# Two layers of graph attention: the second half of a batch's masks and sums moved to later places in the hand-written order

## The chip, the cores and the metric

One core of one Trainium2 chip runs the kernel. The metric is the device time of one execution in microseconds, taken as the median of several runs. The kernel has 64 batches of 256 nodes with 512 features, all in float32. PE is the matrix engine, DVE the vector engine, ACT the scalar engine, POOL is GpSimd, and SP is the engine whose queue issues the DMAs.

## The reference

Layer 0 is a graph attention layer with additive scores; layer 1 is multi-head attention with eight heads of 64 and the same adjacency as mask. Both are behind a layer norm with ReLU and have a residual:

```
h = relu(layernorm(x));  H = h @ W                        # layer 0, W is 512 x 256
e = leaky_relu(H @ a[0] + (H @ a[1]).T, 0.2) + NEG * (1 - adj)
x = x + concat(softmax(e) @ H, H)
h = relu(layernorm(x))                                    # layer 1
q, k, v = h @ Wq.T + bq, h @ Wk.T + bk, h @ Wv.T + bv     # 8 heads of 64
s = where(adj == 0, -inf, q @ k.T / 8)
x = x + (softmax(s) @ v) @ Wo.T + bo
```

## The kernel before, in words

The fast path (`bounded`) computes softmax without subtracting a maximum: scores are bounded, so it takes exponentials, multiplies them by the 0/1 mask, and divides by the sum. Whether the bound holds is judged on the device at the end of the preparation.

Batches are taken in 32 groups g of two (b = 0 and 1). A group passes through four stages, and the stages of different groups run side by side:

- `first_norm` (g + 3): row statistics on DVE (`st`, `mv`), a pair of POOL instructions with a power (`factor`), the normalisation on ACT (`xn`, two tiles per batch), a 32x32 block transpose on DVE (`xt`), a DMA of the blocks to DRAM (`passed`), four DMAs back (`moved`), and a copy on ACT into `hT0`.
- `first_layer` (g + 2): `ph` on PE and its copy into `H` on ACT for four row tiles, with an addition `x<-H,x` on POOL for each; then four transposes `pn` on PE, the scores `e` on ACT and DVE, the products `po`, and the second norm with its own `xn`, `xt`, `passed`, `moved` and `hT1`. The last piece lets POOL make `sums` of `hT1` (`operand_sums`).
- `project` (g + 1): q, k and v by a scheme of seven products of half size each, so 21 products per group. PE writes `pq`, `pk` or `pv`. The intermediate `kept` tiles are copied out of PSUM by ACT into a ring of two buffers; a later addition on DVE reads such a tile, and frees its buffer. A product that adds to a bank waits until that bank was copied.
- attention of g: `scores` (l.716) makes eight `sc` on PE, eight exponentials on ACT into `p` (eight heads, one buffer), four multiplications by `maskT` on DVE (one for a pair of heads, l.735), and four additions on POOL that sum the two halves of the keys (l.736). `weigh` (l.744) makes from `p` the sums `total` and the products `pr`, DVE takes reciprocals `r` and `oT`, and `outputs` (l.777) does seven products `py`, each followed by an addition to `x` on DVE, and stores x.

The order of this work is written out by hand in `steps` (l.874), one string for each b. A letter takes one piece: S is `weigh` of the batch before and `scores` of this one, u a product of `project`, o one of `outputs`, s a piece of `first_layer`, n one of `first_norm`. At the middle letter of a string (l.897) come, for b = 0, the residual additions of `b_out` on POOL (`x<-x,b_out`, four) and the two `value_differences` (`v<-v`) on POOL, and for both b the load of x for g + 3. `scores`, `weigh` and the rest issue their DVE, ACT and POOL instructions as they are called; a scheduler then orders each engine's queue. `not_sooner` (l.123) forbids it to put an instruction ahead of the one issued before it on that engine, and PE's order is a chain throughout.

PSUM has five banks in turn (`mm`) and three that are held. `sc`, `total`, `pr`, `pn`, `ph`, `po` and the second products use the five in turn.

## Time and profile before

| what | value |
|---|---|
| runs before | 2572.51, 2575.55, 2576.94 us; median 2575.55 |
| the profiled execution | 2576.15 us, its span 2574.4 us, granted clock of PE 0.996 |
| DVE masks `p<-p,maskT` 128x1024 | 256, mean 1679 ns, 419.7 us |
| POOL sums `p<-p` 128x512 | 256, mean 1767 ns, 447.3 us |
| POOL `factor` with the power | 128, mean 712 ns |
| ACT exponentials `p<-sc` | 512, mean 609 ns |
| ACT normalisation `xn` | 256, mean 807 ns |
| SP: store of x | 64 of 512 KB, landing 3.1 us after issue |
| SP: `moved` | 496 of 128 KB, landing 3.4 us after issue |

The profile is one execution. The page gives for each engine its busy time and its share of the span; the view of waits says for which engine's work an engine stood idle, how much in total, how often, and the longest; the timeline gives instructions in order of time, merged where equal ones follow each other. All helpers record instructions under two lines (L35 for DVE, ACT and POOL, L137 and L140 for PE), so the names of the tiles tell the rows apart, not the lines. In names the numbers of group and batch are left out.

### The profile page before, as it was taken

Reading aid. Unit: us, or ns where it says so; the run is one execution under the profiler, and the core shown is the slowest. Engines: PE = TensorE matmul, PEld = TensorE weight load, DVE = VectorE, ACT = ScalarE, POOL = GpSimd, SP = SyncE. Lnnn points to the kernel's source line nnn. Section 1 sums busy time; section 2 is a strip of 40 time slices with the busy share of each in tenths; the row PEclk is TensorE's granted clock in tenths of the full one; section 3 lists DMA queues with packets and bytes.
Section 4 is the critical chain, followed back from the end, with each engine's and each line's share of the span. In section 5 each row is a group of like instructions: output and inputs, shape, how many; then the busy total and the mean of one; then the engine's idle time right before and its main releaser. Section 6 shows DMA issues by size and latency. Waiting matters only on the chain.

```text
span 2574.4 us, 41412 instructions
## 1 busy us (share of the span) xinstructions
PE 2508.6 (97%) x16158; PEld 2052.2 (80%) x16158; DVE 1856.3 (72%) x2971; ACT 1014.4 (39%) x2019; POOL 1069.4 (42%) x978
## 2 busy tenths in 40 slices
PE   8999999999999999999999999999999999999997
PEld 7778878888778788788787787887888887878885
DVE  6576766876767877767767678777677676687666
ACT  4443443343343443443433434434434344344321
POOL 3433444334444334443335443344443344433442
PEclk9999999999999999999999999999999999999999
DMA  5122122231232321222312323212223123222000
GB/s 184 66 83 78 55 90 82 91 99 50 74 99 74 99 85 56 82 91 82 99 58 66 99 74 99 85 60 79 91 82 99 64 61 99 83 91 91 33 25 34
DMA packets 129353, 205.40 MB, mean 80 GB/s; under 512 B 13952, under 2 KB 78208, under 8 KB 129152
## 3 DMA queue, kind: packets, MB, share of 16 engines
q1 hardware_dynamic: 129152, 202.69, 24.8%
q8 instruction: 129, 2.11, 0.3%
q14 instruction: 72, 0.59, 0.1%
HBM read 104.08 MB, written 98.57 MB: 79 GB/s over the span
## 4 chain that ended last, share of the span: by engine, by line
PE 87%; DVE 7%; ACT 3%; issue 1%; DMA 1%; SPq 1%; POOL 0%; ACTq 0%; DVEq 0%
PE pk L137 15%; PE py L137 14%; PE pv L137 14%; PE pq L137 13%; PE ph L137 9%; PE sc L137 8%; PE pr L137 7%; PE po L137 4%; DVE p L35 3%; PE total L137 2%; ACT p L35 1%; DMA moved<-passed 1%; DVE r L35 1%; DVE o_sums L35 1%; ACT kept_q L35 1%
## 5 line engine op out<-in xcount | busy, mean ns | idle before, releaser
L35 POOL TENSOR_TENSOR p<-p 128x512 f32<-128x512 f32 x256 | 447.3, 1767 | 528.6 <-DVE p L35 528.6
L35 DVE TENSOR_TENSOR x<-py,x 128x256 f32<-128x256 f32 x448 | 186.9, 417 | 345.1 <-PE py L137 338.6
L35 DVE TENSOR_TENSOR p<-p,maskT 128x1024 f32<-128x1024 f32 x256 | 419.7, 1679 | 0.0
L35 ACT ACTIVATE xn<-x,factor 128x512 f32<-128x512 f32 x256 | 194.4, 807 | 354.6 <-POOL factor L35 354.6
L35 ACT ACTIVATE p<-sc 128x512 f32<-128x512 f32 x512 | 263.2, 609 | 140.2 <-PE sc L137 140.1
L137 PE MATMUL sc<-q,k 64*128 64x256 f32 x2048 | 277.7, 394 | 10.4 <-ACT p L35 10.0
L137 PEld LDWEIGHTS sc<-q,k 64*128 64x128 f32 x2048 | 209.3, 186 | 79.4 <-ACT p L35 28.7
L137 PE MATMUL pq<-hT,wq_sb 128*128 128x256 f32 x1024 | 243.9, 386 | 22.2 <-ACT kept_q L35 22.2
L137 PE MATMUL py<-wo_sb,oT 128*128 128x256 f32 x1024 | 264.4, 381 | 0.4 <-DVE oT L35 0.4
L35 DVE RECIPROCAL r<-total 128x256 f32<-128x256 f32 x128 | 224.7, 1755 | 50.2 <-PE total L137 43.4
L137 PE MATMUL pk<-hT,wk_sb 128*128 128x256 f32 x1024 | 244.9, 382 | 0.0
L137 PE MATMUL pr<-p,v 128*32 128x256 f32 x4096 | 244.5, 379 | 0.0
L137 PEld LDWEIGHTS pq<-hT,wq_sb 128*128 128x128 f32 x1024 | 190.6, 191 | 67.1 <-ACT kept_q L35 33.0
L137 PE MATMUL ph<-w_sb,hT 128*128 128x258 f32 x1024 | 240.6, 383 | 0.3 <-ACT hT L35 0.3
L137 PE MATMUL pv<-wv_sb,hT 128*128 128x256 f32 x1024 | 237.5, 380 | 1.3 <-ACT kept_v L35 1.3
L35 POOL TENSOR_TENSOR factor<-factor,rexp 128x2 f32<-128x2 f32 x128 | 91.2, 712 | 354.4 <-DVE factor L35 354.4
L137 PEld LDWEIGHTS pk<-hT,wk_sb 128*128 128x128 f32 x1024 | 191.7, 190 | 36.1 <-issue 10.7
L137 PEld LDWEIGHTS ph<-w_sb,hT 128*128 128x128 f32 x1024 | 195.2, 191 | 29.9 <-ACT hT L35 0.9
L137 PEld LDWEIGHTS py<-wo_sb,oT 128*128 128x128 f32 x1024 | 195.4, 191 | 29.1 <-issue 1.1
L137 PEld LDWEIGHTS pv<-wv_sb,hT 128*128 128x128 f32 x1024 | 194.9, 190 | 28.6 <-ACT kept_v L35 1.7
L35 ACT COPY hT<-moved 128x512 f32<-128x512 f32 x248 | 141.1, 618 | 188.0 <-DMA moved<-passed 188.0
L137 PE MATMUL py<-wo_sb,o_sums 128*128 128x256 f32 x768 | 200.1, 384 | 8.4 <-DVE x L35 8.4
(122 smaller groups left out, 3789.5 us busy)
## 6 DMA issues: line engine op xcount, KB each, us to landing
passed<-xt SPq DMA_DIRECT2D x124, 512.0 KB, 3.0
moved<-passed SPq DMA_DIRECT2D x496, 128.0 KB, 3.4
x<-in_x_dram SPq DMA_DIRECT2D x64, 512.0 KB, 4.4
out_dram<-x SPq DMA_DIRECT2D x64, 512.0 KB, 3.1
wq_sb<-in_L_gnn_Wq_dram SPq DMA_DIRECT2D x2, 512.0 KB, 8.5
wk_sb<-in_L_gnn_Wk_dram SPq DMA_DIRECT2D x2, 512.0 KB, 10.4
wv_sb<-in_L_gnn_Wv_dram SPq DMA_DIRECT2D x2, 512.0 KB, 7.5
wo_sb<-in_L_gnn_Wo_dram SPq DMA_DIRECT2D x8, 128.0 KB, 4.0
```

The lines of the kernel that those rows point to most:

```text
L35: instruction = getattr(self.engine, operation)(*args, **kwargs)
L137: in_order(nc.tensor.matmul(*args, **kwargs))
```

## The change

The four masks with their four sums leave `scores` and become a generator of four pieces, `mask_pairs`. A new letter m takes one. In both strings two m follow S directly; the third and the fourth stand further back. The mask is now issued through `not_sooner`, too.

```
-            vector.tensor_mul(pair, pair, maskT[:, None, :, :].to_broadcast([P, 2, NT, N]))
-            not_sooner(
-                gpsimd, "tensor_add", pair[:, :, 0, :], pair[:, :, 0, :], pair[:, :, 1, :]
-            )
         places.extend((q_tag, k_tag))
         return p
+
+    def mask_pairs(p):
+
+        for i in range(HP):
+            pair = p[:, 2 * i : 2 * i + 2]
+            not_sooner(
+                vector, "tensor_mul", pair, pair, maskT[:, None, :, :].to_broadcast([P, 2, NT, N])
+            )
+            not_sooner(
+                gpsimd, "tensor_add", pair[:, :, 0, :], pair[:, :, 0, :], pair[:, :, 1, :]
+            )
+            yield
...
-    steps = ("Snuuuuonuouuossnunosunosnouso", "Sususuososuossusuonusonuouunous")
+    steps = ("Smmnuuuuonuouuomssnumnosunosnouso", "Smmsususuososuomssusumonusonuouunous")
...
-                parts = "Snn" + parts[2:].replace("uon", "unon", 1)
+                parts = "Smmnn" + parts[4:].replace("uon", "unon", 1)
...
+                elif part == "m":
+                    next(masks)
                 else:
                     waiting = (g, b, scores(g, b))
+                    masks = mask_pairs(waiting[2])
```

Without its four m the first string is the old one. The second has one s more than before, directly after S and the two m, so each piece of `first_layer` in b = 1 stands one place earlier, and the last s finds nothing left. The middle letter moves with the longer strings: in b = 0 it is now the first of the two s behind the third m.

In the built program the queues of a group in the middle of the run differ as follows.

- DVE, b = 0: the two transposes `xt` of the next norm stand between `o_sums` and the first mask, where they stood around the reciprocal before; two masks; then the additions of q and of three `py`; then masks 3 and 4; then the statistics `st`.
- DVE, b = 1: `o_sums` all stand ahead of the first mask (two masks stood among them); mask 3 stands after the third `py` addition, mask 4 after the v addition and the second pair of `xt`.
- POOL, b = 0: sums 1 to 3, one `x<-H,x`, the four residual additions, the two value differences, one `x<-H,x`, sum 4, the `factor` pair of `first_norm`, two `x<-H,x`. Before: sums 1 to 4, one `x<-H,x`, the `factor` pair, one `x<-H,x`, residual, value differences, two `x<-H,x`. In group 0 the `factor` pair stands ahead of sum 4, and from group 29 on there is none.
- POOL, b = 1: sums 3 and 4 stand behind the two `factor` pairs of the second norm.
- ACT: b = 0 is unchanged, with the two `xn` ahead of the fourth `H` copy; in b = 1 the last two `xn` of `first_norm` stand after the second `hT` copy, directly ahead of the exponentials, and the third and fourth `xn` of the second norm ahead of the first `kept_v`. In group 0, b = 1, both `hT` copies and these `xn` stand ahead of the last `kept_v`.
- SP, around the end of b = 1: `moved` of the second norm stands ahead of the store of x (behind it before), and three of the four `moved` of the next group ahead of the last `passed`; the load of x stands ahead of the last four `moved`.
- PE: the four `po` stand one place earlier among the products of b = 1; otherwise its order is the same.

## The prediction

> **What bounds the kernel now.** I read the page's busy shares first, then the waits of PE, then the timeline of a few groups. Columns of a timeline row: start, duration, engine, operation, out<-in, and in brackets the idle time before it with its releaser.

> ```profile
> span 2574.4 us, 41412 instructions
> PE 2508.6 (97%) x16158; PEld 2052.2 (80%) x16158; DVE 1856.3 (72%) x2971; ACT 1014.4 (39%) x2019; POOL 1069.4 (42%) x978
> ```
> PE is busy for all but 66 us. A gain can only come out of PE's idle time or out of a stage in which PE runs thin; a loss can come from anything that makes PE wait.

> ```profile
> PE pq L137 <- ACT kept_q L35: 22.2, 27, 0.9
> PE sc L137 <- ACT p L35: 10.0, 35, 0.8
> PE py L137 <- DVE x L35: 8.4, 2, 4.2
> ```
> The first row is one wait per group, in the first half (b = 0). The third is the last group, twice.

> ```profile
> 1275.73 2.56 PE L137 MATMUL sc<-q,k 64*128 64x256 f32 x18
> 1282.28 7.84 DVE L35 TENSOR_TENSOR p<-p,maskT 128x1024 f32<-128x1024 f32 x4
> 1290.04 0.68 DVE L35 TENSOR_TENSOR q<-pq,kept_q 128x512 f32<-128x512 f32 x1
> 1290.82 0.84 ACT L35 ACTIVATE kept_q<-pq,bq_sb 128x256 f32<-128x256 f32 x2 [4.01 <-DVE q L35]
> 1291.71 1.99 PE L137 MATMUL pq<-hT,wq_sb 128*128 128x256 f32 x8 [0.59 <-ACT kept_q L35]
> 1295.26 1.03 PE L137 MATMUL py<-wo_sb,o_sums 128*128 128x256 f32 x4
> 1296.67 0.68 DVE L35 BATCH_NORM_STATS2 st<-x 128x6 f32<-128x512 f32 x1
> 1300.95 4.96 POOL L35 TENSOR_TENSOR x<-x,b_out 128x512 f32<-128x512 f32 x4
> 1305.85 2.52 POOL L35 TENSOR_TENSOR v<-v 128x512 f32<-128x512 f32 x2
> 1308.48 0.37 ACT L35 COPY H<-ph 128x258 f32<-128x258 f32 x1 [2.54 <-PE ph L137]
> 1310.87 0.60 PE L140 MATMUL pn<-ident,H 128*128 128x128 f32 x4
> 1316.72 1.56 PE L137 MATMUL sc<-q,k 64*128 64x256 f32 x10
> ```
> One half-group, 1275.73 to 1316.72. Four masks hold DVE for 7.84 us; the q addition behind them frees a `kept` buffer; the third `kept_q` waits for that buffer, and PE waits for `kept_q`. Later POOL does the residual and value rows, and the last H copy ends at 1308.85, 2.02 us before PE's pn.

> ```profile
> 178.19 2.00 PE L137 MATMUL sc<-q,k 64*128 64x256 f32 x16
> 195.95 1.03 PE L137 MATMUL py<-wo_sb,o_sums 128*128 128x256 f32 x4
> 211.56 0.60 PE L140 MATMUL pn<-ident,H 128*128 128x128 f32 x4
> 217.41 1.56 PE L137 MATMUL sc<-q,k 64*128 64x256 f32 x10
> 255.19 1.99 PE L137 MATMUL sc<-q,k 64*128 64x256 f32 x15
> 2374.18 1.13 PE L137 MATMUL sc<-q,k 64*128 64x256 f32 x8
> ```
> Group 1 is undisturbed: 39.22 us for b = 0 (17.76 from sc to the third py, 15.61 to pn, 5.85 to the next sc) and 37.78 for b = 1, together 77.00. Groups 2 to 28 take (2374.18 - 255.19)/27 = 78.48 each. So 1.48 us per group can be won in b = 0.

> **The change part by part.** No instruction is added or removed; DVE, POOL, ACT and SP get other orders.

> *Two masks instead of four after the scores.* The q addition stands behind two masks. In the row above masks started 6.55 us after sc; in the built order the two transposes xt come before them (1.3 us), while the four o_sums, at 1.5 us each beside POOL's sums, shorten as sums start earlier (next item). By these rows the q addition comes about 8 us after sc instead of 14.3, and the third product whose `kept_q` needs the buffer ends only 10.7 us after sc. The wait goes.

> *b = 1 one piece earlier, and the hT rows fetched ahead of the store on SP.* The rows moved1 no longer stand behind the store that waits for a py addition, so the hT copy (1276.77 here, after 4.80 us of idling for its DMA, with the exponentials right behind it) needs DMAs issued some 3 us earlier: passed is issued at 1263.99 and lands in 3.0, moved in 3.4 (page), so at 1270.4. The copy then follows the v copy (ends 1271.97) and ends 2.7 us before sc; xn (1.52 us) ends 1.2 before it, and the exponentials start 1.16 after it, as in group 1. The passed rows of the next group move the other way on SP, behind the masks' transposes: about 7 us later. With 3.0 and 3.4 us to land they are there some 12 us after sc (wanted by their hT copy at 22), the last quarter of the other half at 9.5 (wanted at 12), and the load of x in between on SP lands in 4.4, some 10 us before its statistics. Covered. With both items b = 0 runs like group 1: -1.48 x 27 = -40.0 us.

> *Masks 3 and 4 behind the third py addition: a new chain to pn.* On POOL, the third sum now stands before the residual rows, the fourth sum behind the value rows, and the pow pair of the next norm behind that. ACT has xn before the last H copy, and the fourth pn transpose needs that copy. Worked from py (= a): mask 3 starts at a+1.41, where the statistics start now. How mask pairs and sums run back to back is shown in b = 1:

> ```profile
> 1325.83 2.35 DVE L35 TENSOR_TENSOR p<-p,maskT 128x1024 f32<-128x1024 f32 x2
> 1327.12 3.42 POOL L35 TENSOR_TENSOR p<-p 128x512 f32<-128x512 f32 x2 [1.83 <-DVE p L35]
> ```
> The first of these sums takes 2.19, the second 1.26. So sum 3 lets its successor start 3.45 after mask 3. Then POOL, start to start: H row 0.60, residual and value rows 7.36 (1300.95 to 1308.31), H row 0.69, sum 4 1.22, pow pair 0.97: a+15.70. Then ACT: 0.03 to xn, 1.43 to the copy of H, 0.37, and 0.05 to PE: a+17.58. PE wants the fourth transpose at a+15.61+0.33 = a+15.94. New wait: 1.64; the first matmul after a wait takes 0.1 more (1.99 for 1.89 in the pq row): 1.74 us. It is in groups 1 to 28 (in group 0 the pow pair stands ahead of sum 4; from 29 on there is no norm): +1.74 x 28 = +48.7 us. Bounds: 0.8, if sum 3 got ahead of mask 4 and took 1.26; 2.7, if sum 4 too were held for 0.93. I take 1.74, from rows of the same pairs. Behind the waiting xn on ACT stand the H copy, kept_k and the e rows, which keep their distance from pn; behind the waiting xt on DVE stand two py additions, the later needed 0.3 us after it ends.

> The trace decides who waits: mask 4 starts before mask 3 ends, and sum 3 pays 0.93. [...]

> *Masks 3 and 4 in b = 1.* They stand among the v addition and the xt transposes. By the rows' durations sum 4 ends 26 us after sc, wanted at 33, and the first kept_v ends 1.5 us before PE's third pv: nothing.

> *Ends.* Group 29 gains 1.4 and has no chain. Group 30 gains 1.3, but its value rows come at a+12.3 where pr wants them at 10.3: +0.8 net. Group 31 waits 4.2 us twice for DVE x behind four masks; with two masks the addition comes as PE arrives, and the slow matmuls after the wait go too (2.07, 1.91 and 1.87 for 1.03). A wait of 1.6 behind masks 3 and 4 comes instead: about -8.7 for both halves. Group 0: in b = 1 ACT now has the second hT copy before the last kept_v, which delays it by about 3 us: +2.5.

> *Sum.* -40.0 + 48.7 - 1.4 + 0.8 - 8.7 + 2.5 = +1.9 on the profiled execution's 2576.15, which is 0.6 above the median of 2575.55: 2577.5 against that median.

> **The rivals.** 0.2% is 5.15 us, about what a measurement of this kernel can tell from no change.

> *The wait at pn lowers PE's clock (slower).* A wait of 2.69 us was followed by eight matmuls at half rate:

> ```profile
> 86.57 3.05 PE L137 MATMUL pv<-wv_sb,sums 128*128 128x256 f32 x8 [2.69 <-ACT kept_v L35]
> 89.41 2.57 PE L137 MATMUL pv<-wv_sb,hT 128*128 128x256 f32 x8
> 2529.00:2531.00 2.00, 1.56 (x4) 1.29 (x5) 0.81 (x3) 0.00 (x0) 2.00 (x2) 0.50 0.00 0
> ```
> The last row is a stretch after a 4.21 us wait; its granted clock (third figure from the end) is 0.50. Waits of 1.1 and 1.3 us (160.8 and 169.2) were followed by full rate. So the point lies between 1.3 and 2.7, and 1.64 may pass it. Price: 8 x 0.215 = 1.7 us per group, +48: 2626; in half the groups 2602.

> [...]

> *The gain stays away (slower).* If xn, now directly before the exponentials, or a late DMA holds them, b = 0 keeps half of its 1.48: +20, 2598; all of it: 2618. Against it: 2.4 us of slack on ACT between xn and the exponentials.

> *No wait at pn, or half of it (faster).* If sum 3 gets in first: 0.93 x 28 less, 2551. If the pow pair does not hold ACT at all: 2577.5 - 48.7 = 2529. Against it: POOL's order is fixed in the program and its rows repeat to 0.02 us in groups 2 to 28.

> *Nothing moves.* The built orders do move; only if all terms are hidden: 2575.

> **How the numbers follow.** Main case 2577.5, own range 2566 to 2590 (a tenth of a microsecond in the chain is 2.8 us): 0.46, of it 0.07 faster, 0.24 same, 0.15 slower. Clock: 0.14. Gain away: 0.18. Faster rival: 0.18, of it 0.01 same. Nothing moves: 0.04, of it 0.03 same, 0.01 slower. Faster 0.24, same 0.28, slower 0.48. The range leaves a tenth on each side: 2550, as the lower half of the faster rival lies below, and 2614, as the full price of the clock and of the missing gain lie above.

> **What would show it.** Right: the row pq <- kept_q gone from PE's waits; a row pn <- ACT H in its place, some 28 times, 1.4 to 1.8 us each, about 45 us; 17.8 us from sc to the third py in every group; xn on ACT waiting for POOL factor; the py <- DVE x waits of the last group below 2 us. Wrong: no pn wait (the chain is shorter), pn waits followed by a granted clock of 0.5 (clock rival), or sc and pq waits still there (gain away). A wait at pv or at ph in the steady groups would be one that I have not seen.

## The result and the profile after

| | median | runs |
|---|---|---|
| before, same chip | 2574.82 us | 2572.51 to 2576.94 (4) |
| after | 2572.10 us | 2571.69 to 2574.16 (4) |

The ratio is 0.9991, with a 95% interval of 0.9974 to 1.0009: no change that can be told from none. The profiled execution of the changed kernel took 2571.85 us (span 2570.2, granted clock 0.998), 4.3 less than the one before. First the head of its page, then its waits of PE (in total, times, longest).

```profile
span 2570.2 us, 41394 instructions
PE 2490.8 (97%) x16158; PEld 2052.6 (80%) x16158; DVE 1691.7 (66%) x2971; ACT 1012.5 (39%) x2019; POOL 1008.7 (39%) x978
```
```profile
PE pn L140 <- ACT H L35: 41.2, 29, 1.5
...
PE sc L137 <- ACT p L35: 8.0, 31, 0.3
PE pv L137 <- ACT kept_v L35: 7.8, 3, 4.9
PE py L137 <- DVE x L35: 3.1, 2, 1.7
```
The row pq <- kept_q (22.2 us) is gone; a row pn <- ACT H, once in each of groups 0 to 28, has taken its place. The half-group that the prediction showed of before, now of after (timeline: start, duration, engine, operation, and in brackets the idle time ahead with its releaser):

```profile
1278.71 3.92 PE L137 MATMUL sc<-q,k 64*128 64x256 f32 x32
...
1283.72 2.32 DVE L35 TENSOR_TENSOR p<-p,maskT 128x1024 f32<-128x1024 f32 x2
...
1286.39 0.69 DVE L35 TENSOR_TENSOR q<-pq,kept_q 128x512 f32<-128x512 f32 x1 [0.35 <-PE pq L137]
...
1296.48 1.03 PE L137 MATMUL py<-wo_sb,o_sums 128*128 128x256 f32 x4
...
1297.89 2.35 DVE L35 TENSOR_TENSOR p<-p,maskT 128x1024 f32<-128x1024 f32 x2
1299.25 2.12 POOL L35 TENSOR_TENSOR p<-p 128x512 f32<-128x512 f32 x1 [10.86 <-DVE p L35]
...
1301.92 4.94 POOL L35 TENSOR_TENSOR x<-x,b_out 128x512 f32<-128x512 f32 x4
...
1309.97 1.26 POOL L35 TENSOR_TENSOR p<-p 128x512 f32<-128x512 f32 x1
...
1311.19 0.70 POOL L35 TENSOR_TENSOR factor<-factor,rexp 128x2 f32<-128x2 f32 x1
...
1312.20 1.52 ACT L35 ACTIVATE xn<-x,factor 128x512 f32<-128x512 f32 x2 [6.46 <-POOL factor L35]
...
1313.62 0.35 ACT L35 COPY H<-ph 128x258 f32<-128x258 f32 x1
...
1314.03 0.32 PE L140 MATMUL pn<-ident,H 128*128 128x128 f32 x1 [1.44 <-ACT H L35]
...
1319.60 1.56 PE L137 MATMUL sc<-q,k 64*128 64x256 f32 x10
```
The scores run without a stop (3.92 us), and the q addition comes as soon as PE has its product. Then the new chain: mask 3, sum 3, residual and value rows, sum 4, factor, xn, H, and PE's fourth pn 1.44 us late. Per group 2 to 28 the first sc stand 78.64 us apart, 78.48 before. From the third py on, b = 0 takes 1.66 us more (from pn to the next sc 7.51, before 5.85). Without it a group would take 76.98: so 1.50 was won, and 1.66 lost.

### The profile page after: what moved, and what is told of

Read it like the earlier page. It is cut to its first block, busy times and chain, and to the rows that moved or that the text cites. A ratio compares the mean times of both kernels' runs of the same rounds, so it can differ in the third digit from the quotient of the medians.

```text
span 2570.2 us, 41394 instructions
## 1 busy us (share of the span) xinstructions
PE 2490.8 (97%) x16158; PEld 2052.6 (80%) x16158; DVE 1691.7 (66%) x2971; ACT 1012.5 (39%) x2019; POOL 1008.7 (39%) x978
## 4 chain that ended last, share of the span: by engine, by line
PE 77%; POOL 14%; DVE 3%; issue 3%; ACT 2%; DMA 1%; POOLq 0%; SPq 0%; DVEq 0%; ACTq 0%
PE pq L137 15%; PE pv L137 15%; PE py L137 12%; PE sc L137 10%; PE pk L137 9%; PE pr L137 8%; POOL x L35 6%; PE po L137 4%; POOL p L35 4%; POOL v L35 3%; PE total L137 2%; DVE p L35 2%; ACT xn L35 1%; POOL factor L35 1%; PE ph L137 1%
## 5 line engine op out<-in xcount | busy, mean ns | idle before, releaser
L35 POOL TENSOR_TENSOR p<-p 128x512 f32<-128x512 f32 x256 | 407.8, 1603 | 970.9 <-DVE p L35 881.0
L35 ACT ACTIVATE p<-sc 128x512 f32<-128x512 f32 x512 | 264.0, 612 | 211.2 <-PE sc L137 203.3
L35 ACT ACTIVATE xn<-x,factor 128x512 f32<-128x512 f32 x256 | 194.4, 806 | 387.1 <-POOL factor L35 387.1
L35 DVE TENSOR_TENSOR x<-py,x 128x256 f32<-128x256 f32 x448 | 186.4, 416 | 243.8 <-PE py L137 234.6
L35 DVE TENSOR_TENSOR p<-p,maskT 128x1024 f32<-128x1024 f32 x256 | 301.5, 1209 | 0.0
L137 PE MATMUL sc<-q,k 64*128 64x256 f32 x2048 | 266.5, 390 | 8.0 <-ACT p L35 8.0
L35 DVE RECIPROCAL r<-total 128x256 f32<-128x256 f32 x128 | 224.8, 1756 | 66.3 <-PE total L137 59.9
L137 PE MATMUL py<-wo_sb,oT 128*128 128x256 f32 x1024 | 262.8, 379 | 3.5 <-DVE x L35 3.1
L137 PEld LDWEIGHTS sc<-q,k 64*128 64x128 f32 x2048 | 213.0, 186 | 62.1 <-issue 25.9
L35 DVE STREAM_TRANSPOSE xt<-xn 128x512 f32<-128x512 f32 x248 | 164.4, 692 | 134.2 <-ACT xn L35 134.2
L137 PE MATMUL pr<-p,v 128*32 128x256 f32 x4096 | 245.5, 379 | 0.4 <-POOL v L35 0.4
L137 PE MATMUL pk<-hT,wk_sb 128*128 128x256 f32 x1024 | 244.9, 382 | 0.0
L137 PE MATMUL pv<-wv_sb,hT 128*128 128x256 f32 x1024 | 238.6, 381 | 4.9 <-ACT kept_v L35 4.9
L137 PE MATMUL pq<-hT,wq_sb 128*128 128x256 f32 x1024 | 239.9, 382 | 0.0
L137 PE MATMUL ph<-w_sb,hT 128*128 128x258 f32 x1024 | 239.4, 381 | 0.3 <-ACT hT L35 0.3
L137 PEld LDWEIGHTS pv<-wv_sb,hT 128*128 128x128 f32 x1024 | 195.3, 191 | 32.2 <-ACT kept_v L35 5.3
L137 PEld LDWEIGHTS pk<-hT,wk_sb 128*128 128x128 f32 x1024 | 191.7, 190 | 36.1 <-issue 10.7
L137 PEld LDWEIGHTS pq<-hT,wq_sb 128*128 128x128 f32 x1024 | 191.8, 190 | 35.0 <-issue 9.9
L137 PEld LDWEIGHTS py<-wo_sb,oT 128*128 128x128 f32 x1024 | 193.8, 190 | 32.3 <-DVE x L35 3.9
L137 PEld LDWEIGHTS ph<-w_sb,hT 128*128 128x128 f32 x1024 | 194.4, 190 | 29.6 <-ACT hT L35 0.9
L137 PEld LDWEIGHTS pr<-p,v 128*32 128x32 f32 x4096 | 133.3, 110 | 88.6 <-POOL v L35 0.9
L35 POOL TENSOR_TENSOR factor<-factor,rexp 128x2 f32<-128x2 f32 x128 | 91.7, 716 | 281.2 <-DVE factor L35 281.2
## 6 DMA issues: line engine op xcount, KB each, us to landing
wk_sb<-in_L_gnn_Wk_dram SPq DMA_DIRECT2D x2, 512.0 KB, 10.7
```

What stands on the lines that cost most here:

```text
L35: instruction = getattr(self.engine, operation)(*args, **kwargs)
L137: in_order(nc.tensor.matmul(*args, **kwargs))
```

## The experiments

Each kernel is measured beside the kernel before on the same chip. Where a string has a new letter R, the work of the middle letter (residual additions, value differences, the load) stands at R, so that it keeps its place when letters ahead of it move. (In b = 1 of the two kernels without the additional s, R, which there moves only the load, stands two letters ahead of the old middle; the order on SP is that of the kernel before all the same.) The string of group 0 is fitted in the same way. "b = 0" and "b = 1" are the two strings; times per group are means of groups 2 to 28, from one first sc to the next.

### Which part brings the 1.50 us

Four kernels differ only in the strings. All four masks back behind S in b = 0:

```
-    steps = ("Smmnuuuuonuouuomssnumnosunosnouso", "Smmsususuososuomssusumonusonuouunous")
+    steps = ("SmmmmnuuuuonuouuossRnunosunosnouso", "SmmsususuososuomssuRsumonusonuouunous")
```

> All four masks of b = 0 stand directly behind S again, the middle letter's work where it was before the change; b = 1 as in the changed kernel. It separates the two items of the gain. If the gain of 1.48 us per group comes from the second string alone (hT copies and xn earlier, exponentials on time): scores in 3.85 us, no pq wait although four masks stand ahead of the q addition, no pn wait, 76.98 us per group; with 4.5 us back in the last group about 2530 us. If the two masks carry the larger part, as the prediction's first item has it: the pq <- kept_q wait of 0.8 us is back in 27 groups, about 2552 us.

Measured: 2533.19 us, ratio to before 0.9839 (0.9825 to 0.9852). The profile has 77.01 us per group, 3.85 from the first sc to the next product in every group, and neither a pq <- kept_q nor a pn row. Four masks ahead of the q addition hurt nobody once the exponentials are on time; the gain needs nothing from the first string.

The other way round: b = 0 as in the changed kernel, b = 1 as before.

```
-    steps = ("Smmnuuuuonuouuomssnumnosunosnouso", "Smmsususuososuomssusumonusonuouunous")
+    steps = ("SmmnuuuuonuouuomsRsnumnosunosnouso", "SmmmmususuososuossRusuonusonuouunous")
```

> b = 0 as in the changed kernel (two masks, then two later); the string of b = 1 and its four masks as before the change, without the additional s. If the second string frees the scores: sc is late again by a mean of 0.70 us as before (4.55 for 3.85), pq <- kept_q stays away because only two masks stand ahead, the pn wait of 1.66 stays: 2572 + 27 x 0.70 + 4.5 for the last group, about 2595 us. If the masks of b = 0 carry the whole gain: 3.85 us for the scores, 2576 us.

Measured: 2589.32 us, ratio 1.0054 (1.0039 to 1.0070). The pq wait stays away, the scores are late again (3.86 to 5.35 us, mean 4.36 for 3.85), the pn wait stays: 79.17 us per group. ACT ahead of the scores, in the timeline of this kernel:

```profile
1285.55 1.14 ACT L35 COPY hT<-moved 128x512 f32<-128x512 f32 x2 [4.85 <-DMA moved<-passed]
1286.59 4.00 ACT L35 ACTIVATE p<-sc 128x512 f32<-128x512 f32 x8
```
PE has begun its sc at 1284.46, and the exponentials stand behind an hT copy that waits for its DMA. So two masks alone take away the pq wait, but not this delay.

The second string holds two edits, the additional s and the later masks 3 and 4. The s alone, with four masks behind S in both strings:

```
+    steps = ("SmmmmnuuuuonuouuossRnunosunosnouso", "SmmmmsususuososuossuRsuonusonuouunous")
```

> Nothing of the masks moves: all four stand directly behind S in both halves, as before the change. Only the one s more in the second string is left of it. If that s is the whole gain: groups 2 to 28 at 76.98 to 77.00 us with scores in 3.85 us, no pq wait, no pn wait, and about 2533 us as with four masks in the first half alone. If masks 3 and 4 behind o_sums in b = 1 carry part of it (four masks at up to 1.96 us ahead of the reciprocal ri in b = 1): scores or pk late in b = 1, 0.5 us or more per group, 2547 us or more.

Measured: 2585.54 us, ratio 1.0041 (1.0027 to 1.0055): slower than before by 0.4%. b = 0 is at its 39.22 us, but b = 1 takes 39.34 for 37.79, so that a group takes 78.56, as good as before; groups 0 and 1 lose 8.1 and 1.5 us on top (89.17 and 78.54 for 81.10 and 77.01). The waits of PE, then DVE, ACT and PE in one b = 1 of this kernel:

```profile
PE pv L137 <- ACT kept_v L35: 45.7, 33, 5.0
```
```profile
1330.48 6.77 DVE L35 TENSOR_TENSOR p<-p,maskT 128x1024 f32<-128x1024 f32 x4
1337.17 0.15 DVE L35 RECIPROCAL ri<-po 128x1 f32<-128x1 f32 x1
...
1347.28 1.52 ACT L35 ACTIVATE xn<-x,factor 128x512 f32<-128x512 f32 x2 [2.33 <-POOL factor L35]
1348.70 0.56 ACT L35 COPY kept_v<-pv 128x512 f32<-128x512 f32 x1
...
1349.32 1.99 PE L137 MATMUL pv<-wv_sb,sums 128*128 128x256 f32 x8 [1.21 <-ACT kept_v L35]
```
The same place in the kernel with the split masks in b = 1 (four_masks_first_half; its scores begin at 1295.89, here at 1325.53):

```profile
1314.23 1.52 ACT L35 ACTIVATE xn<-x,factor 128x512 f32<-128x512 f32 x2 [0.47 <-POOL factor L35]
1315.66 0.56 ACT L35 COPY kept_v<-pv 128x512 f32<-128x512 f32 x1
...
1317.90 1.89 PE L137 MATMUL pv<-wv_sb,sums 128*128 128x256 f32 x8
```
The additional s puts the last two xn of the second norm ahead of the first kept_v on ACT. With four masks in front, DVE reaches the second norm's statistics late (the reciprocal ri ahead of them starts 11.64 us after sc, with two masks 7.52), and this kept_v starts 23.17 us after sc; with two it starts at 19.77, ahead of PE's pv at 22.01. So the later masks pay for the earlier piece. The fourth combination, later masks without the s:

```
+    steps = ("SmmmmnuuuuonuouuossRnunosunosnouso", "SmmususuososuomssRusumonusonuouunous")
```

> Masks 3 and 4 of b = 1 stand later as in the changed kernel, but the second string has no additional s, and b = 0 has its four masks directly behind S. With it the four combinations in b = 1 are complete. If the s is needed (the moved rows then still stand behind the store of x on SP, and the hT copy ahead of the exponentials is late): scores at 4.0 to 5.4 us and the pq wait of 0.8 us as before the change, 78.5 us per group, about 2573 us. If the later masks alone are enough, because DVE reaches the second norm some 2.4 to 4 us earlier: 3.85 us, 77.0 us per group, about 2533 us.

Measured: 2576.38 us, ratio 1.0007 (0.9998 to 1.0016). Scores late by a mean of 0.80 us, the pq wait back (17.4 us), 78.71 per group. SP in this kernel, then in the changed one, a little ahead of the scores of b = 0 (they begin at 1276.96 and 1278.71):

```profile
1265.74 0.38 SPq L35 DMA_DIRECT2D passed<-xt  x1
1271.39 0.40 SPq L823 DMA_DIRECT2D out_dram<-x  x1
1271.89 3.13 SPq L457 DMA_DIRECT2D moved<-passed  x4
```
```profile
1264.28 0.34 SPq L35 DMA_DIRECT2D passed<-xt  x1
1267.82 1.73 SPq L457 DMA_DIRECT2D moved<-passed  x4
1273.13 0.40 SPq L823 DMA_DIRECT2D out_dram<-x  x1
```
Without the s, the four moved are issued behind the store of x, 6.2 us after passed, and the hT copy idles 4.81 us for them; with it they are issued 3.5 us after passed, ahead of the store. Over the whole run ACT's hT copies wait 12.6 us for DMA in the changed kernel, 199.5 here.

Together, with four masks behind S in b = 0:

| b = 1 | no additional s | additional s |
|---|---|---|
| four masks behind S | 2574.8 (before) | 2585.5 |
| masks 3 and 4 later | 2576.4 | 2533.2 |

Neither edit is worth anything alone; the two together are worth 41.6 us.

### What the wait at pn hangs on

Only mask 4 of b = 0 one letter on, behind the factor pair (the first string alone is shown):

```
-    steps = ("Smmnuuuuonuouuomssnumnosunosnouso",
+    steps = ("Smmnuuuuonuouuomssnunmosunosnouso",
```

> Only mask 4 of b = 0 moves one letter on, so that sum 4 (1.22 us) stands behind the factor pair on POOL and sum 3 stays ahead of the residual rows. My theory (the chain is sum 3, residual, value, sum 4, factor, xn, H copy): the wait shrinks from 1.66 by 1.22 to about 0.45, 28 x 1.2 less: 2538 us. Rival (it is a single late thing such as sum 3 held by mask 4, or the DVE statistics): the wait stays whole (2572) or goes whole (2526).

Measured: 2544.44 us, ratio 0.9883 (0.9868 to 0.9898). The pn row shrinks from 41.2 to 11.1 us; from pn to the next sc it is 6.43 us, so 0.58 of the 1.66 are left. Sum 4 was worth 1.08 us in the chain (1.22 expected). By subtraction the rest is sum 3 ahead of the residual rows; the next kernel moves that one too.

Masks 3 and 4 both behind the factor pair (again the first string):

```
-    steps = ("Smmnuuuuonuouuomssnumnosunosnouso",
+    steps = ("Smmnuuuuonuouuossnunmmosunosnouso",
```

> Masks 3 and 4 of b = 0 stand together behind the statistics and the factor pair instead of ahead of them; b = 1 as in the changed kernel. My theory (the wait at pn comes from sums 3 and 4 ahead of the factor pair on POOL): the pn wait of 1.66 us goes in groups 1 to 28, 78.64 - 1.66 = 76.98 us per group, 2572.1 - 28 x 1.66 = 2526 us. Rival (a wait takes its place, because the py7 and pk additions now stand behind two masks of 1.21 us): 0.5 to 2.4 us per group come back, 2540 to 2593 us, with a row py <- DVE x or pk <- ACT kept_k in PE's waits.

Measured: 2555.30 us, ratio 0.9922 (0.9909 to 0.9936). The pn wait is gone and b = 0 has its 39.22 us, but b = 1 takes 38.67 for 37.76. A wait did take its place, though not the one I had named. Waits, and the place in the timeline of this kernel:

```profile
PE sc L137 <- DVE r L35: 16.5, 27, 0.7
PE sc L137 <- DVE oT L35: 15.8, 27, 0.6
```
```profile
1303.94 1.78 POOL L35 TENSOR_TENSOR x<-H,x 128x256 f32<-128x256 f32 x2
...
1304.00 2.26 DVE L35 SCALAR_TENSOR_TENSOR e<-e 128x512 f32<-128x512 f32 x2
1306.19 1.75 DVE L35 RECIPROCAL r<-total 128x256 f32<-128x256 f32 x1
```
The same DVE pair in the kernel with four masks first:

```profile
1291.88 1.38 DVE L35 SCALAR_TENSOR_TENSOR e<-e 128x512 f32<-128x512 f32 x2
```
Sum 4 now delays the last two H rows of POOL, and they meet the e rows on DVE. Side by side both took longer than in the kernel with four masks first (the e rows 2.26 us for 1.38, the H rows 1.78 for 1.32). The reciprocal behind them is 0.88 late, and the scores of b = 1 wait twice for it and its product, 0.58 us each.

### How near the clock rival was

POOL gets two more instructions behind sum 3 of b = 0, so that pn waits longer. They add the second half of the keys to a sum and take it off again (`mask_pairs` is given b for it). The three kernels differ in the slice (`:, 0, k, :P`, then `:, 0, k, :`, then `:, :, k, :`):

```
+            if b == 0 and i == HP - 2:
+                half, other = (pair[:, 0, k, :P] for k in range(2))
+                not_sooner(gpsimd, "tensor_add", half, half, other)
+                not_sooner(gpsimd, "tensor_sub", half, half, other)
```

> The changed kernel with two POOL instructions of 128 x 128 behind sum 3 of b = 0, about 0.35 us each by half of those of 128 x 256, so that the wait at pn is about 2.15 us, between the 1.45 of the changed kernel (matmuls at full rate behind it) and the 2.82 with two of 128 x 256 (total and pr at half rate behind it, 1.6 us more). If the limit lies above 2.15: 2572.1 + 28 x 0.7 = 2592 us. If it lies below: 28 x 1.6 = 45 us more, 2637 us.

> The changed kernel with two more POOL instructions of 128 x 256 (the second half of one head is added to its sum and taken off again) behind sum 3 of b = 0, 0.6 us each by the H rows, so that the wait at pn grows from 1.45 to about 2.7 us. If a wait of this size leaves the granted clock alone: 2572.1 + 28 x 1.2 = 2606 us, with the matmuls behind pn at 0.215 us of 128x256 for two. If it halves the clock for eight matmuls, as behind the 2.69 us before pv in the kernel before: 1.7 us more per group, 2654 us.

> The same with two instructions of 128 x 512, 1.22 us each by sum 4: the wait at pn grows to about 3.9 us. Without a change of the clock: 2572.1 + 28 x 2.44 = 2640 us. With eight matmuls at half rate behind each wait: 48 us more, 2688 us, and a granted clock of about 0.5 in the stretch behind pn.

| | pn wait | groups 1 to 28 with slow matmuls behind it | mean cost of these in all 28 | time |
|---|---|---|---|---|
| changed kernel | 1.45 us | 0 | 0 | 2572.1 |
| 128 x 128 twice | 2.27 | 16 | 0.94 us | 2625.0 |
| 128 x 256 twice | 2.82 | 24 | 1.41 | 2659.7 |
| 128 x 512 twice | 3.90 | 28 | 1.95 | 2711.0 |

The cost is the time from the fourth pn to the next sc above the 5.57 us that it takes in the changed kernel. Where it is paid it is 1.63 to 1.69 us for waits of 2.27 and 2.82. Longer waits and slow matmuls together give 28 x (0.82 + 0.94) = 49, 28 x (1.37 + 1.41) = 78 and 28 x (2.45 + 1.95) = 123 us; 53, 88 and 139 were measured, and most of the rest of the last is in groups 0, 30 and 31, which take 6.8, 4.4 and 2.7 us more than in the changed kernel. With the shortest pause, two groups that follow each other, each after a wait of exactly 2.27; first the timeline, then the stretches behind pn (length, busy time, and third from the end the granted clock):

```profile
215.47 0.32 PE L140 MATMUL pn<-ident,H 128*128 128x128 f32 x1 [2.27 <-ACT H L35]
...
217.63 2.96 PE L137 MATMUL pr<-p,v 128*32 128x256 f32 x32
```
```profile
296.57 0.32 PE L140 MATMUL pn<-ident,H 128*128 128x128 f32 x1 [2.27 <-ACT H L35]
...
298.14 1.91 PE L137 MATMUL pr<-p,v 128*32 128x256 f32 x32
```
```profile
216.00:218.00 2.00, 2.00 (x16) 0.59 0.62 252
```
```profile
297.00:299.00 2.00, 2.00 (x28) 1.00 0.58 231
```
The price was as the rival had it, and the waits at which it began lie between 1.45 and 2.27 us; but there was no one length. The same wait of 2.27 us cost 1.6 us in one group and nothing in the next, and the share of the groups that paid grew with the wait, from 0 to 16, 24 and 28 of 28.

The records of the granted clock in the traces show what decided. In each of the twelve, every drop of the granted clock starts on a grid of steps of 3.413 us, and lasts one step or two (the last one runs into the end of the trace). In the kernel before, the five drops start 6, 709, 7 and 6 steps apart; in the changed kernel the three start 24 and 703 apart. The grid lies elsewhere in each execution: the first drop starts 87.35 us into the span before, 85.25 after. Here are the steps of the grid, called windows, that hold the two waits, each with the window behind it:

```profile
212.94:216.35 3.41, 1.15 (x8) 1.00 0.00 0
216.35:219.76 3.41, 3.41 (x30) 0.50 0.78 303
```
```profile
291.44:294.86 3.41, 2.86 (x15) 1.00 0.00 0
294.86:298.27 3.41, 1.70 (x17) 1.00 0.12 50
298.27:301.68 3.41, 3.41 (x72) 1.00 0.69 259
```
The first wait lies within one window: PE idles for 2.26 of 3.41 us, and the next window has half the clock. The second is cut in two, 0.55 and 1.71 us, and nothing follows. Between the first sc and the last product the twelve traces hold 93 windows at full clock that a window at half clock follows; each has 1.92 us of idling or more. The 8510 that one at full clock follows have 1.88 or less. (In the kernel before and the changed one alone, 4 windows with 2.49 to 3.30 us, and 1438 with up to 1.66.) So in these traces it was the idling within a window that counted. By these figures a wait of 1.45 us by itself was too short wherever it fell, one of 3.90 left at least 1.95 in one window however it was cut, and for those between it depended on where the grid cut them.

### A version without the wait

Only in the last group was the split of b = 0 worth something. So: four masks behind S everywhere, two and two in b = 0 of the last group.

```
+            if g == NG - 1 and b == 0:
+                parts = "SmmnuuuuonuouuomsRsnumnosunosnouso"
```

> As with four masks in the first half, but in the last group b = 0 takes two masks and then two, as in the changed kernel. In the last group the split is worth what the traces show: 17.07 for 21.40 us in b = 0 and 23.49 for 23.89 in b = 1, so 4.7 us less: 2533.2 - 4.7 = 2528.5 us. Rival (the last group's gain came from the groups ahead of it): 2533 us, unchanged.

Measured: 2528.68 us, ratio 0.9823 (0.9810 to 0.9837), faster than the kernel before and the changed one. The last group, up to the end of PE's last product, takes 40.55 us, 45.29 with four masks; groups 2 to 28 take 77.01 as with four masks.

## Why the prediction was right, and where it was not

2577.5 was forecast, 2572.1 came: within 0.2% of before, as the main case had it, and inside its own range. More weight lay on slower, for rivals that didn't come.

- *The chain to pn* was right link by link. From the third py (1296.48): sum 3 frees POOL after 4.85 us, the last H row before sum 4 starts after 12.81 (12.82 worked out), xn at 15.72, the fourth pn at 17.55 (17.58). The effect was 1.66 us per group for 1.74. Sum 3 did pay for mask 4: it took 2.12 us, while mask 4, which had begun 0.23 us ahead of it, kept its 1.22. The experiment that moved sum 4 alone took 1.08 us of it away.
- *The gain of 1.48 us per group* was right as a sum: 1.50. Its working was not. The step "Two masks instead of four after the scores. [...] The wait goes" was true of the wait (old_second_half has no pq row), but the gain did not need it: with the exponentials on time, four masks did no harm. And the step "Masks 3 and 4 in b = 1 [...] nothing" missed what this shift carries. I priced what it costs, not what would happen without it: the earlier piece of the first layer would have cost 1.5 us per group at pv. That the sum fitted all the same was luck in this term: the change happened to carry both halves of the gain. The step "b = 1 one piece earlier, and the hT rows fetched ahead of the store on SP" had the right mechanism, shown by the SP rows above, but holds only together with the other.
- So the split in b = 0 was the loss of this change, and the split in b = 1 with the s its gain. I had put the first on both sides of the account.
- *Ends.* Group 1 paid 1.63 as the others did. Group 29 won 1.4, as forecast; group 30 lost 0.5 (0.8 forecast); group 31 won 9.1 up to PE's last product (8.7). Group 0 took 81.76 us for 81.10, +0.7 where +2.5 was forecast, and its scores began 1.1 us sooner. Within it b = 1 lost 4.5, and this belongs to the order: b = 1 of group 0 takes 44.7 to 48.7 us in all nine kernels with the additional s, and 40.3 to 40.9 in the three without it. It is the delay that was forecast, only larger: PE waits 4.92 us at pv for a kept_v that stands behind the second hT copy on ACT. b = 0 won 3.8, and a granted clock that dropped or not made 2.6 there by itself (40.13 for 37.51), with one and the same order (last section). That the term came out small is luck.
- *The sum*: 0.7 - 1.1 + 1.6 + 27 x 0.16 - 1.4 + 0.5 - 9.1 = -4.5, and 0.3 more behind PE's last product make -4.2, against -4.3 of the profiled executions; +1.9 was forecast. Of the difference 2.9 are group 0 and its start, and some 2.7 the 0.1 us per group by which chain and gain were mis-sized.
- *The clock rival* did not come: 0 of 28 groups. The step "So the point lies between 1.3 and 2.7, and 1.64 may pass it" looked for a limit on the length of a wait. In the twelve traces a drop followed 1.92 us or more of idling within one window, and no window of groups 1 to 29 of the changed kernel has more than 1.47. With 0.8 us more of wait it came in more than half of the groups. *The gain stays away* did not come, and for a reason that I had not seen, the split in b = 1. *No wait at pn* did not come.
- What was to show it, did: pq <- kept_q gone; pn <- ACT H 29 times, 41.2 us; 17.77 us from sc to the third py in every group; xn waiting for POOL's factor; the py <- DVE x waits at 1.7 and below.

## What to carry to other kernels

When one diff moves several things, build the four combinations of the two that touch the same stretch: here each alone was worth nothing or less, and together 41.6 us. Before a moved instruction is priced at nothing, ask also what else in the diff relies on its move. And an instruction moved behind a late result should be followed on the queue that it joins: two sums on an engine that is 39% busy cost PE 1.66 us per group, because a short instruction on the way to PE stood behind them.

## What the runs showed of the hardware

```profile
110.00:120.00 10.00, 10.00 (x37) 0.77 0.26 86
```
```profile
110.00:120.00 10.00, 10.00 (x48) 1.00 0.20 60
```
  The same wait, the granted clock 0.77 and 1.00, and 37 matmuls for 48 in ten microseconds: in the one 2.49 us of the wait fall into one window, in the other the grid cuts it into 1.45 and 1.84. b = 0 of group 0 took 40.40 us in the one and 37.51 in the other. In split_in_last_group, whose order is the same as with four masks up to the last group, it took 40.13.
- In the kernel before a mask beside a sum on POOL took 2.29 us for 1.21, and a sum beside a mask 2.18 for 1.26. In the changed kernel 255 of the 256 masks took 1.18 to 1.22 us (mean of all 1209 ns, 1679 before): 118 us less of DVE's time. The sums beside them still paid, 96 of 256 with 2.1 to 2.2 us. PE had no gain from the shorter masks: with four masks in the first half 63 masks take 2.3 us again, and a group takes 77.01.
